# A four-layer convolution sequence: GpSimd's additions wait for the VectorE operation ahead of a port operation, in a new written order

## The chip, the cores and the metric

The kernel runs on one core of a Trainium2 chip. The core has TensorE (matrix products, with a separate path for loading weights), VectorE (elementwise work and scans), ScalarE (activation functions, copies), GpSimd (here: elementwise additions) and SyncE, which issues DMA transfers. The profile calls them PE, PEld, DVE, ACT, POOL and SP. Each engine works through its own queue in order, and waits on semaphores that other engines raise. The metric is the device time of one execution in microseconds (us), as the median of several runs.

## The reference

Four layers work on an input of 4 images of 128 channels x 64 x 64 points, in 32-bit floats:

- Layer 0 is attention over the 4096 points of an image: queries and keys of 16 channels, `softmax(q k)`, values of 128 channels, the result scaled by gamma and added to x.
- Layer 1 is a residual block of two 3 x 3 convolutions (two of the nine taps are masked) with weights and activations quantized to 4 bits.
- Layer 2 is a Mamba block. Two projections to 256 channels, a causal convolution of two taps, `silu`, then a selective scan over the 4096 points with 16 states per channel:

```
h = exp(dt * A) * h + dt * B * x
y = sum over the 16 states of h * C
```

  Then `(y + x D) * silu(z)` is projected back to 128 channels, normalized in groups, put through `silu` and added to the input.
- Layer 3 is attention with 64 channels for queries, keys and values, with an output projection.

## The kernel before

All layers of all four images are in flight together. The work is written as 19 generators ("chains"), such as `energies`, `exponentials`, `products` (attention), `convolutions` (layer 1), `preparation`, `decays`, `scans`, `additions`, `output` (layer 2), `fetches` (DMA). Every step of a chain is one small piece of work on one engine. In which order the steps are issued is written out by hand, as it were: the constant `SCORE` is a string of 9,949 letters, each letter a chain (`n` is `scans`, `o` is `additions`, `i`, `j`, `k` the attention chains). `Order.run` walks through the string and takes the next step of the named chain. The order in which the instructions of one engine are issued follows from this string; the times given to `op(...)` in the code are not used in the kernel (they belong to whatever made the string), and nothing is planned at run time. Attention runs first for images 0 to 2, and in the last stage, layer 3 of image 3, nothing else is left.

Layer 2 is the part that the change touches. It goes in pieces of 512 points (the first two pieces of image 0 have 256). For a piece and two of the 16 states at a time (a "pair"), with both halves of the 256 channels in one tile:

- L1311, on VectorE, multiplies `ud` (dt times x) by the fetched row `b_n` into `hs`, 128 x 2048 elements: the *product*.
- L1285, on ScalarE, makes the decays `exp(dt A)` in PSUM. L1331, on VectorE, is the scan, 128 x 512 elements at a time, two for each state.
- L1348, on VectorE, multiplies `hs` by the fetched row `c_n`: the *readout*. It is issued between the two scans' pairs of the next pair, so that VectorE's pattern is: product, two scans, readout of the pair before, two scans.
- L1359, on GpSimd, adds one state of `hs` to `y`, 128 x 1024 elements: the *addition*, two for each pair. After the 16th state L1363 multiplies `y` by `sz`, the *gating product*.

`hs` has three buffers, so a product waits until the additions of the pair three before are done. `y` has two.

Operations of VectorE marked `port=True` are called *port operations* here: the products and readouts, and in layers 1 and 2 also L938, L950, L977, L984, L987, L1139, L1142, L1144, L1148 and L1226. Right after issuing one of them the code calls `held`, which remembers it. When GpSimd's next addition or gating product is issued, `behind` makes it wait for the remembered operation, by a semaphore. So a GpSimd operation starts only once the last port operation issued before it is done, and runs beside what VectorE does next, in most cases two scans. The calls, at lines 894 to 902, 1311, 1348, 1359 and 1363:

Of the kernel before, what the change touches and what calls it, by code (L numbers as in the profile page):

```python
# [74 lines left out]
    "finish3": "CDEFGHIJ",  # L75
# [4 lines left out]
ittiiuccbvaauitatiaiswjaijaiiukuiviajkajiitkwtiikjijkikcuuisjbbibjkbbittikjjidkikuujiikjibbxcjik  # L80
xxkxbajijabjikkikjjiidxkjayyyykijyieeesejkibjseeiceeceeeekfjkffkijfikffkjjiifdxfjfffxkjxffffpffk
xiixpesfkjkfeffjenlnmlnnfmniinpekfellhmjfnnknenomjoifjkfinhmnlnnmjeifkdlijenpyneylnommjkkihlneyi
eefsnjojknnnflnlhmmffopnnnnfiinkynfkkjiyomlmhjnfpnoonnojlfiknpnjflfmfnonnsmfhkldffnoffkxxnnnxlol
mfppxxnehkfiinenfffejmnnjofekiehlneofmelnjmnnonnikejieneesjflkmeikohjmlnnijpnnijlnophmmnkfflkons
nnodiynijnnyppjmylflfhmkkinjoonnifjfnolflnnnommhnnkfpffkifnnnlnfmhmjokpgonlnnifngjllnfhmfonnnfmn
nikfjffylfmlhpyfmiiokfkdonnonnnnjofkfpfhfknjisljmijfnnonkkploinmnipjjkklnonomnfiikjjhinolkjdfimj
nxnikfxfxxlpnnkxfppjxmoxkkenehenmlijonijeelnmkniijpeeokenhjlnneeeiiemknojnjlfppfnhmkpiodnjinnjfo
kkflkmnnfkflinnmnijhjponppflfmknoniinjogfjklimjgijhnnlkfnokffmndypnpijffnyyfylkkpnyymynflhiejmff
onennokkffijffieejekhkmieelnijnfeenopkinejlmjkndiikjjnloihpneiknjmpnopnklkojpinmfnjikhklnnfomnne
oijflpiknfjkisjfpmdnxjlnmnnoxhpnoiffxjxkkpiljxmiffjnnogklxxmhiisknnojgffkgpennlfefkjifnemopnnejo  # L90
limhiennkjfnpejklnpmfofdiijelnfmkknfnhjoninifjflgnjmnkkijikkjplmpohnifinnonjjkklmnfdijonyffeeffe
ipheenkkjmlnnyykypiiyyojyjffkiijkkknejelopmnnnpmklninhjoiejiipjsdelkjnnompiiknelnhmnffonklnmonnf
fejjkppnfkifpilofmnhnnjjoekflmnzffknnggglpniokotzzzmitudenuxhnelneieeoivmittpfnufuhnmlnpiiwntpit
xxolununxxmfffnflxxmopneheoffffffinnnefeepfelnimtntponeveeesieelomuuniwneefijkhnliifnojjmnijpnln
pkhomiijnneeeejlpkknmnonpkiefelmeeopjnnhfkinijjlmknnkidijmkonlnnfkffsijohljimpnnfjkijkijnoeplenh
pnffmokipljnnoofnfkiimlgnjggkmnknfpnofdyphlnnyfikmfynyoyyjmylpnnonhfnkijjfpfkflmijnonnijlkijkmnn
ophijpkeiiljfkfnmekjonnfpffldmnpoehnnnijiffekifjfpklkjnmnkiikejofnlmphnonnjkiijkjefkofldxnmnijxx
xpnijhlmnkonkiikexjnxxlmonknsijikjjippnlfkjffmennfphijoinlfnmnoefkjlmnhnpopnnofffokidigfkglfmfgp
jnnjhnmfklepoekeiifnnjnpjkelonkimnnpffielojjmkfnffhinijknlonmkdynjeklneepeiyikyyeoyhnmjpnnpyjkif
ylnfoijmkkjneielnihjnkjmiinjjolnmeeeeonnffkfffkpiednppoijjeflkkhnmienenjifkmelpjnokkiijnknjiiljm  # L100
jnhonnklkdmxnpnoijinopjlnkxxxkfmnksxfxpiixhlnnkjmfjofinejnilnjohmnepenoopkfkiiffjlkmffgnkpngeefd
kglnjiiemonhnnepjmoljnkfnfelfkijnfmfnhokifipnnkjipjlmikjfjfkonnnlmfpnfonhkdlnnfeiijmyjeokknlipim
nkpnnojikjhjeenepoilijkjnmnpffiifkffnyyjkyykiydljhmnynkokijifjkklnesjemijonnpnilnmnpfeoekeenpjol
mkiinneknjljepneomkdnxffnepeiijkofxxmfplnxjnkenffxijiopkxxmlknjineljnijpnfkmifonejilkkgmnonnnooj
fgkfmlngeeippnsdelnjmnnpikfoeijfknifjijjfflekkinmonifkfnjklmnnojpffkfnlpiimnonnfjlkndmynjeeioeek
kjlymiyyispenynppkyjjoiikkfjynfffeefnjkfilnjeemneoenkiiljemnkepndkjomlniijhnnpofnkjkilisoenmnjkk
pneofjilmfipjnjhnlnkzfkfmfonnlfpenitkpthimdnxpuxunzxonffiilnvtitxxxiexolzzuumenwimentfitugnounfi
phgngipfgvttfloiggnmniuuoplwffffijnmonghiigjjlnnpknmfnfkoiifeljenmjnnpflhonekepiimfjopnkejlnknii
pkhjmijnjelnonmeeeinoggponffggeffikkfdggkggggggeejglgnjgnkgeeesmgknggeihijkkjlngpgiinokmejknpjlg
nghkpmdnyoiiejjgenijyilkyyykmnegeeynnyfokfijjijkpnkmlnniiheofknjoffjmlnppfinenoijlmknsjfhfnnkoio  # L110
igfdjkjfpmplngkffkgfniglfmhnieefnnjonjiikelekpmoenjnknjlmhoinnpnjifkklfjmopfiidnxnjxnlnmffnjkkox
hfpknpxxxpolmfixnjnijlenphkeomnknijnifjpffkffmiljknknofnpieojeidljhmnnnijeekkkoliijkjmknnnfiflij
jpmhkkeoknnpnildnjmnyioejepnelosypynkiiykyhjmyynkjinijlfkfmjfkffnnpoeeminphoilnkejnffmklnnfjoini
ejlghnjngmnkefoedipnepeoifgslmkfojekknnnpffmeiholjennienkjjemlnfipiojnffkkpnplfhomnjnknieffflkjd
iixnmnonpkjxlxxxnojkxmnxihijjlkefnkkmenonffiifjeeppfjfehknilmknpnionejjijkdlnoijmipnnokkijlifneh
mnnkjjkoeilmeiknkfppnnfjleejsonmnifhniokjjplnfkfmdyinepnijfopljkfyfmkyyhyiinlnfmjnpoyyjneeokgnkk
fgflmgnofhnnfnilimnnjkefpejieiojlmfknnnffhokpnjlmideppiojfkkfjifnnnlnmhjniojlnfmkkiijjkninliksfp
onohmpknnnjjlmokdpnnxfffffnpeikxxxkjijleijmnknhelijoffnexmninkjkijkopnmloijnkhnpnlopkxndmiinxene
jjlnkkiimhnjjkkponepiiflkjknomnenpfjmhfslnnfoknppiijjflkfmfdnynonifljhggmnonnooijikjelyyngyeymne
pikyfyfphlkffnomfnnnelnipofffjmpnjfffehkklnnmenioepneeijlkjnmnoeisijnflkjkidnomhpnneiejjolkfkknm  # L120
nffffkiijefejempepniiplokkhnejnnjezekeflpomknzznnlniimnhvonwliopdxnviminnfwlnfxfimznfhvopenlnfmo
infwxpfifenvhxospmlnnnoofxwlgmingjijpnxxliijgnnmnjhkkkkifofppnikjlkffnmofkipjlfkfnnnhfmnonkfijif
kplnjmokifnnjjkdloidimhjpjennnmelfnkkponkkkknopifjmlhijnfeeijpennfijfflkkkfeokijmnnkkiiddpnjkplj
mehkoiiennnjklpeekknjskmioniCljnhnjiiomnjnfflmnnCkkkokkpjkldpijenifmodhnfnnppjijklomknniienfplkk
fkjmknnhonojklnfiiemknpnjkfjlinhoimnnjppjofkkkfilnmddijnjglengkkkhmnfnonpokfkkflmfpnAiinnjejlehe
mnofnnoijffflmnniiffefkppkjCilkkCChfnCpmnonnooeCkkjjCidCdfgjmklfnnkfffkijijfenhlnkkkminopjepnelo
ikjfCksknDmDniipjkkkenjliioddknjkmpnnpkijlijkjnmkflkiionnmnnjjofkknfplmnnofifjieplnfpfmonnnkjifo
kkojflgfinifpgmkgjfflnmDnonDnnDDDiDjBddilnkkomnDkkklpkmpnojjfnnnfffiljmnifnkkiffoEkEppnjlmonnkkj
pkfflndiijEndikEomjkknknilpEmoEjpiEFjnnnkkkolnFijmnfffjDAffkkinjloiEnEpmfjpnEikknkjiidldmFFkojnn
jnkoklphFmnnnkkiFFiBfjlnFjkkmnFppiiojjlnnkkipjmoinffhknflfnomnkfpjfkdlmhnffioinnnojojlgdgiimnffk  # L130
gppkkjngklggknfpfiomhnjkjnnklnffmiiffnojklkjijmnpfpfFinnAfhofnkkloGGmnnnkddjlnphmofninGGjpplnikk
kkomGkGinGjkjlGmGhijijnnnggpokknfkffkiikfkgjiddlfjkmfHoGnnHnkjlnkoihmpjijnHniiHHkkHHBookflnmpnji
jlgHjmpHnnnohgngkkgggggggpggmgiglkkfkoknnifjfpjggnifidggodlmnfgjkkfnjgkhilgmpnfgpngknoHjfkgkknfo
fiflgfmhnjnifglkgnomjkijfffnlppnmknnionjfkkffpihniddIIlpkmjojIInnhimlnniknpfokjkjnmiiklnfIjnkljk
onphmkkijijnolnniomkppAkkjiIiddIjkknnnlnmnjhfoknpffifIflInijjkkkmnkoiinjjfkklzhmopkknkddnzznittl
noJpiuimulJvinhtInpJtinouuzBiimngJfoJpwntlimtunuJnopnJiolvinmftthniflununpffiomfnwfifjlmnffhngpn
ofglkJnmJijnoffnijlkmhippnnojfijnmknlfffnonijplnhnomnkfkpifjinjfklmiJpjijnkknfdionhlnojippmnjkln
mnkijfionnkjlmikjnknoppffhfnfpijmikjlkfkdnyoinnpijkjijlnikyyyykomynyjiihnkjlefmennjlonmhopkijfkn
neeiienelmjkoppkdijjnnlhmnnokennpkffiiljjonkmffnnpkiljmhionnnpjffikjlmgnfkpfkfnflonmohnnngooikgj
dxffijgmlxikixxxpnkjxknjfxnmlnpipofehjfnneiijkfmpljfinnkojfnfkomlnnfiihnkkjojmlpfdnfnneifffiekkp  # L140
jhmejlfonnneppkiikjijlmjoninneljknkkimikjodnyhlemeneepjenyoyinkyykyijynijkklppnmioneejlhinnjokej
fmfenlpinpneimokjfkffinhnlnojmneijfklnopdmjhnnfifkjnooelnfkfmgkiffigfnmglpkfpenhnnjjlioneeminpjj
kfkfnlonnffpijimnjophneekkldfxonmnfijfnikkxxjiolnmhnixxpknojjlxkxnipimjfnkkfekenlffpfejmeinjlnki
dehjoikffjkknmfenpfopiinneeojlkmihpnnjeiknejjmkipeoljinlnmnknijkjndlhyyyyiioekkmnppyjnjynhloynmk
npofenniijoflkjfpnkmnenifijfjmkpoflhnnijnijfloofkmfnnggkfiihfgdlpkfennjmnfejkeonleomneffflknppni
infkojminjhnoplfinkkjkmnnijliopnfmfnhjplnkdxjnmnoneiexxjliejepekfknoxxkimijxxlenkkeehenfpjffiifk
jkponmnijfnlhmenknijdikofnjlkpijimjennopnlenmkkojheeinnpjmiljpknfonnkiijljkfiknomfnhpjfenedfmyii
lnoknejjyfknfyyyiioyylnppmnkfhnjjelnfmnpofekfgkinglmnniohnffjjmlnnkoepigojieejnelmnfhokfkiniffdj
jefppnlfokfmnnnpkijflnieemkjhfnkiiojneekkejfplffmnkkzzzzndpxiiolvimnxxnnohwfnlviifpxxmownvnnoilp
miwhfnnnivwxxlnpmiiojjiilnnkefkpepnokmnnpolnjjmleeneniikomkjkfkjknnnfifmolnnppejnijlofmnnnoikjkk  # L150
# [37 lines left out]
class Order:  # L188
# [32 lines left out]
    def run(self):  # L221
        for voice in SCORE:
# [7 lines left out]
            if item[1] is None:  # L230
                self.chains.pop(voice)
# [27 lines left out]
def conv_seq_kernel(ctx: ExitStack, tc: tile.TileContext, i: dict, out: bass.AP):  # L259
    nc = tc.nc  # L260
# [1637 lines left out]
```

## Time and profile before

| What | Value |
| --- | --- |
| Median of 3 runs | 3256.88 us (3255.39 to 3258.67) |
| The profiled execution's own time | 3258.73 us |
| Its span, first to last instruction | 3256.9 us |
| Mean granted TensorE clock | 0.983 |
| TensorE busy | 3075.6 us, 94% |
| VectorE busy | 2942.3 us, 90% |
| ScalarE busy | 2550.4 us, 78% |
| GpSimd busy | 1298.7 us, 40% |

A row of a group in the profile reads: line, engine, operation, output and input tiles with their shapes, number of instructions, then after the bar the busy time, the mean of one in ns, and after a second bar the time in which the engine was idle before them, and what ended most of that. A row of waits reads: who waited for whom, in total us, how often, the longest. A row of the timeline reads: start, duration, engine, line, operation, and how many instructions were merged into it. The chain of work that ended last follows the work back from the last instruction.

Busy time is the time in which an instruction is open on its engine. An instruction that has been started and then has to wait for something inside the engine still counts as busy.

### The profile page before, as it was taken

How to read it: one execution, taken by the hardware profiler on the slowest of the kernel's cores; microseconds unless marked ns; L12 is line 12 of the kernel's file. 1: busy time of each engine (PE TensorE's matmuls, PEld its weight loads, DVE VectorE, ACT ScalarE, POOL GpSimd, SP SyncE). 2: the span in 40 equal slices, each digit the busy share in tenths (PEclk: the TensorE clock that was granted, in tenths of full speed). 3: DMA queues.
4: the chain of work that ended last, by engine and by line, in shares of the span. 5: the costliest groups of instructions: out<-in, count | busy, mean ns of one | idle time of the engine just before them, and what ended most of it. 6: DMA issues, size and time to landing. Idle time of an engine off the chain costs nothing. (4 is left out here: it accounts for less than half of the span.)

```text
span 3256.9 us, 69082 instructions
## 1 busy us (share of the span) xinstructions
PE 3075.6 (94%) x29404; PEld 2260.7 (69%) x29404; DVE 2942.3 (90%) x2377; ACT 2550.4 (78%) x3734; POOL 1298.7 (40%) x582
## 2 busy tenths in 40 slices
PE   8989989999899999999898999999899999999998
PEld 7878858888688887555556878865566555565665
DVE  3699999999999999999999999999999999993554
ACT  5888878888788887888787888878888888875554
POOL 0244444444344444444444444444444444450000
PEclk9999999999999999999999999999999999999999
DMA  2233333233333334333333222233333333330000
GB/s 71 81 99 106 102 118 104 96 108 105 108 117 103 104 102 131 105 109 117 111 130 127 99 98 93 97 125 109 104 125 114 133 114 113 119 108 11 2 11 22
DMA packets 134878, 321.67 MB, mean 99 GB/s; under 512 B 44384, under 2 KB 55072, under 8 KB 134560
## 3 DMA queue, kind: packets, MB, share of 16 engines
q1 hardware_dynamic: 134272, 316.32, 28.9%
q8 instruction: 232, 3.80, 0.5%
q10 hardware_dynamic: 288, 0.85, 0.1%
q14 instruction: 86, 0.70, 0.1%
HBM read 300.35 MB, written 16.78 MB: 97 GB/s over the span
## 5 line engine op out<-in xcount | busy, mean ns | idle before, releaser
L1359 POOL TENSOR_TENSOR y<-y,hs 128x1024 f32<-128x1024 f32 (+1 forms) x528 | 1220.0, 2311 | 1569.1 <-DVE hs L1311 644.6
L659 ACT ACTIVATE p<-e 128x1024 f32<-128x1024 f32 x1024 | 1016.4, 1019 | 183.5 <-PE e L641 161.7
L1331 DVE TENSOR_TENSOR_SCAN hs<-da,hlast,hs 128x512 f32<-128x512 f32 (+1 forms) x928 | 1124.7, 1249 | 36.6 <-ACT da L1285 15.8
L723 PE MATMUL us<-v,p 128*128 128x129 f32 x8192 | 1012.9, 280 | 23.7 <-ACT us L780 11.2
L723 PEld LDWEIGHTS us<-v,p 128*128 128x128 f32 x8192 | 964.5, 194 | 81.4 <-ACT p L659 16.8
L1285 ACT ACTIVATE da<-dt,late 128x512 f32<-128x512 f32 (+1 forms) x1056 | 705.5, 677 | 303.4 <-DVE hs L1331 292.0
L1311 DVE TENSOR_TENSOR hs<-ud,b_n 128x2048 f32<-128x2048 f32 (+1 forms) x264 | 620.0, 2348 | 6.3 <-POOL y L1359 4.2
L1348 DVE TENSOR_TENSOR hs<-hs,c_n 128x2048 f32<-128x2048 f32 (+1 forms) x264 | 590.8, 2238 | 4.5 <-DMA c_n<-bc_d 2.3
L641 PE MATMUL e<-it,v 64*128 64x256 f32 x4096 | 531.6, 396 | 21.7 <-ACT p L659 21.3
L732 PE MATMUL us<-p,v 128*32 128x256 f32 x8192 | 501.8, 383 | 4.7 <-ACT p L659 4.1
L641 PEld LDWEIGHTS e<-it,v 64*128 64x128 f32 x4096 | 373.1, 188 | 162.4 <-issue 74.8
L732 PEld LDWEIGHTS us<-p,v 128*32 128x32 f32 x8192 | 246.2, 110 | 216.5 <-issue 53.3
L641 PE MATMUL e<-it,j 64*128 64x256 f32 x2048 | 208.8, 313 | 24.5 <-ACT p L659 19.3
L641 PEld LDWEIGHTS e<-it,j 64*128 64x128 f32 x2048 | 142.7, 186 | 88.0 <-ACT p L659 31.6
L751 PE MATMUL us<-p,ones 128*32 128x256 f32 x3072 | 202.6, 381 | 0.0
L681 DVE TENSOR_TENSOR acc<-p,acc 128x1024 f32<-128x1024 f32 x96 | 117.5, 1224 | 39.3 <-ACT p L659 32.5
L751 PEld LDWEIGHTS us<-p,ones 128*32 128x32 f32 x3072 | 96.1, 110 | 72.9 <-issue 13.2
L1331 DVE TENSOR_TENSOR_SCAN hs<-da,hs 128x512 f32<-128x512 f32 (+1 forms) x128 | 133.2, 1074 | 7.0 <-ACT da L1285 4.4
L1028 PEld LDWEIGHTS <-w 128*128 128x128 bf16 x594 | 53.1, 98 | 85.8 <-issue 43.9
L1028 PE MATMUL xh<-x,w 128*128 128x512 fp8e4 (+1 forms) x396 | 94.7, 375 | 14.0 <-ACT xc L1074 6.7
L1363 POOL TENSOR_TENSOR y<-y,sz 128x1024 f32<-128x1024 f32 (+1 forms) x33 | 75.9, 2301 | 71.4 <-DVE hs L1348 54.8
L681 DVE TENSOR_TENSOR acc<-p 128x1024 f32<-128x1024 f32 x16 | 19.6, 1224 | 83.1 <-PE ss L694 44.4
(173 smaller groups left out, 2563.6 us busy)
## 6 DMA issues: line engine op xcount, KB each, us to landing
b_n<-bc_d SPq DMA_DIRECT2D x256, 512.0 KB, 3.7
c_n<-bc_d SPq DMA_DIRECT2D x256, 512.0 KB, 3.7
x_in<-in_x SPq DMA_DIRECT2D x16, 512.0 KB, 6.1
xpad<-in_x SPq DMA_DIRECT2D x32, 256.0 KB, 4.6
x_d<-yo SPq DMA_DIRECT2D x24, 256.0 KB, 2.1
x_in<-x_d SPq DMA_DIRECT2D x12, 512.0 KB, 5.1
o<-x_d SPq DMA_DIRECT2D x24, 256.0 KB, 4.0
out<-o SPq DMA_DIRECT2D x24, 256.0 KB, 4.2
```

The costliest lines, as they stand in the source:

```text
L641: nc.tensor.matmul(e[h][:, k % 2, k // 4, :], lhsT=jts[s][row : row + D3, col : col + P], rhs=its[s][row : row + D3, c * CB : (c + 1) * CB ...
L659: nc.scalar.activation(p, es[t][h], AF.Exp)
L681: nc.vector.tensor_add(accs[k], ps[t, h], other)
L723: nc.tensor.matmul(us[:, r, 0:VP], lhsT=ps[t, h][:, k % 2, k // 4, r * P : (r + 1) * P], rhs=vts[s][:, 8 * q + k, :], start=q == 0 and k = ...
L732: nc.tensor.matmul(us[m : m + 32, 0, :], lhsT=vts[s][:, 8 * q + k, m % D3 : m % D3 + 32], rhs=ps[t, h][:, k % 2, k // 4, :], start=q == 0 ...
L751: nc.tensor.matmul(us[32 * m : 32 * m + 32, 1, :], lhsT=ones[:, 0:32], rhs=term, start=False, stop=q == NQ - 1 and k >= len(terms) - 4,)
L1028: nc.tensor.matmul(g, lhsT=w3[:, k // len(rhs), lhs[k % len(rhs)] : lhs[k % len(rhs)] + P], rhs=x[:, rhs[k % len(rhs)]], start=(k == 0), s ...
L1285: nc.scalar.activation(da, live["in", g][0][:, h, :], AF.Exp, scale=amat[:, h, n : n + 1])
L1311: held(nc.vector.tensor_mul(hs, live["in", g][1].unsqueeze(1).to_broadcast([P, 2, 2, T]), bcs.pop(("b", k)).unsqueeze(2).to_broadcast([P, ...
L1331: nc.vector.tensor_tensor_scan(hs[:, m % 2, h, :], das.pop((m, h)), hs[:, m % 2, h, :], hlast[:, n, h : h + 1] if index[g] else 0.0, ALU.mult,
L1348: nc.vector.tensor_mul(hs, hs, bcs.pop(("c", k))[:, a:b].unsqueeze(2).to_broadcast([P, b - a, 2, T]))
L1359: behind(nc.gpsimd.tensor_tensor(y, y, hs[:, m % 2], ALU.add))
```

## The change

Two things are changed. First, `held` now remembers two operations: the port operation, and the VectorE instruction issued just ahead of it. A new sign `~` in the string sets `order.early` for the next step; a GpSimd operation issued under that sign waits for the instruction ahead of the port operation in place of the port operation itself. Second, the string is a new one, of 10,350 characters, 401 of them `~`; the other 9,949 name the same steps of the same chains as often as before, but for the voices of one chain (`finish3` now shares its steps among five letters in place of eight), and in another order.

```diff
-    "finish3": "CDEFGHIJ",
+    "finish3": "CDEFG",
...
-ittiiuccbvaauitatiaiswjaijaiiukuiviajkajiitkwtiikjijkikcuuisjbbibjkbbittikjjidkikuujiikjibbxcjik
...
+iCqjiCqqjqiCjijikEkkCjkqqjAiidkrkjkjkidiqCCqqCjjqCiikjqkjkkqqrGCddDDDDDDDDCBDD
...
         self.locks = {True: None, "h": None}
+        self.early = False
...
         for voice in SCORE:
+            if voice == "~":
+                self.early = True
+                continue
             item = self.chains[voice]
...
             if item[1] is None:
                 self.chains.pop(voice)
+            self.early = False
...
     def held(inst):
-        holders[:] = [inst]
+        ahead = next(
+            k
+            for k in reversed(nc.cur_bb.bb.instructions)
+            if k is not inst.ins and k.engine == inst.ins.engine
+        )
+        holders[:] = [ahead, inst.ins]
 
     def behind(inst):
-        for holder in holders:
+        for holder in holders[:1] if order.early else holders[1:]:
             tc.add_manual_dep(
-                inst.ins if hasattr(inst, "ins") else inst,
-                (holder.ins if hasattr(holder, "ins") else holder).name,
+                inst.ins,
+                holder.name,
```

An addition still waits for the readout whose result it adds, so the early wait can only be used when another port operation has been issued after that readout. In the new order 113 additions that stood right behind their own readout have become 72; the others stand one or more port operations later. Of the 401 early operations, 175 are held ahead of a product, 108 ahead of a readout, 118 ahead of the other port operations. The lines of the kernel after the change are higher by 9 to 14 (L1311 is L1325, L1331 is L1345, L1348 is L1362, L1359 is L1373).

## The prediction

> **What bounds the kernel now.** I read the page's busy shares first, then the three stages, then the costliest groups and VectorE's list of waits, and last single stretches in order of time.
>
> ```profile
> PE 3075.6 (94%) x29404; PEld 2260.7 (69%) x29404; DVE 2942.3 (90%) x2377; ACT 2550.4 (78%) x3734; POOL 1298.7 (40%) x582
> ...
> 0.00:112.00 112.00, 102.35 (x815) 87.05 (x816) 43.61 (x119) 70.98 (x97) 2.83 (x19) 1.00 0.23 69
> 112.00:2940.00 2828.00, 2668.77 (x24959) 1973.68 (x24957) 2744.41 (x2099) 2312.74 (x3413) 1295.50 (x564) 0.98 0.33 110
> 2940.00:3257.00 317.00, 304.52 (x3633) 200.02 (x3633) 154.28 (x160) 166.67 (x225) 0.36 (x1) 0.98 0.03 11
> ```
>
> The lower rows are stretches: length, then busy time of TensorE, its weight loads, VectorE, ScalarE, GpSimd. From the first scans (112 us) to GpSimd's last product (2940 us) VectorE is busy for 2744 of 2828 us, 97%, TensorE for 94%. After 2940 us only TensorE is near full. So VectorE sets the pace of the middle, with TensorE close behind; GpSimd is idle half of it.
>
> ```profile
> L1359 POOL TENSOR_TENSOR y<-y,hs 128x1024 f32<-128x1024 f32 (+1 forms) x528 | 1220.0, 2311 | 1569.1 <-DVE hs L1311 644.6
> ...
> ACT da L1285 <- DVE hs L1331: 292.0, 357, 2.9
> ...
> DVE hs L1331 <- ACT da L1285: 20.3, 29, 1.7
> ...
> DVE hs L1311 <- POOL y L1359: 4.2, 24, 0.3
> ```
>
> ScalarE's decays wait 292 us for VectorE's scans, the reverse is 20 us: VectorE leads. What of VectorE's busy time is a hidden wait shows only in time order:
>
> ```profile
> 2515.52 2.26 DVE L1348 TENSOR_TENSOR hs<-hs,c_n 128x2048 f32<-128x2048 f32 x1
> 2517.70 2.45 DVE L1331 TENSOR_TENSOR_SCAN hs<-da,hlast,hs 128x512 f32<-128x512 f32 x2
> 2517.93 2.36 POOL L1359 TENSOR_TENSOR y<-y,hs 128x1024 f32<-128x1024 f32 x1 [2.38 <-DVE hs L1348]
> 2520.07 2.37 DVE L1311 TENSOR_TENSOR hs<-ud,b_n 128x2048 f32<-128x2048 f32 x1
> ```
>
> The readout ends at 2517.78. The addition that waited for it starts 0.15 later and ends at 2520.29, 2.51 after the readout. The two scans beside it end at 2520.15. The next product, recorded from 2520.07, ends 2.29 after the scans, where the first one here ended 2.18 after the scans ahead of it: 0.11 us inside its busy row is a wait for the addition. In every such case it ends 2.15 us after the addition. Summed over all rows of port operations with an addition still running under them, VectorE loses 65.9 us so: 210 waits of up to 0.35 us make 31.4, 27 larger ones 34.5. The larger ones are nearly all a second addition on the same port operation (38 such).
>
> **The change, part by part.** No instruction is added to VectorE (2,379 in both orders), GpSimd has the same 561 additions and products and SP the same DMAs; only semaphore targets and places differ. In the built order 401 of the 561 wait for the operation ahead, 160 still for the port operation (or for nothing of VectorE's).
>
> *What an early wait is worth.* Twice before already, an addition came just after a port operation had begun:
>
> ```profile
> 2573.11 2.27 DVE L1348 TENSOR_TENSOR hs<-hs,c_n 128x2048 f32<-128x2048 f32 x1
> 2573.16 4.44 POOL L1359 TENSOR_TENSOR y<-y,hs 128x1024 f32<-128x1024 f32 x1
> 2577.67 2.36 POOL L1359 TENSOR_TENSOR y<-y,hs 128x1024 f32<-128x1024 f32 x1
> 2578.05 4.13 DVE L1311 TENSOR_TENSOR hs<-ud,b_n 128x2048 f32<-128x2048 f32 x1
> ```
>
> The readout ended at 2575.38, unharmed at its usual 2.27; the addition ended at 2577.60, 2.22 after it. (The other: an addition at 2888.54 took 4.47, the product under it ended at 2890.79, again 2.22.) So an early addition ends 2.22 after its port operation where a late one ends 2.51 after: 0.29 us gained. The next product needs the port two scans later, 2 x 1.17 (median from end to end) + 0.03 = 2.38 after a readout. Late costs 0.13, early nothing, with 0.16 to spare. After a product L1311 the first scan ends 0.21 later than usual (it reads what L1311 wrote), so there even a late addition (2.51) fits before 2.59.
>
> Here the skill speaks against the change: the Trainium skill, "SBUF — State Buffer", section "A bandwidth-pool intuition that's wrong", has GpSimd's blocked work proceed only at "DVE-end + ~115 ns". With 115 ns and then a whole addition of 2.36, it would end at 2.48, 0.03 better than late. The rows say 2.22; I take the rows, and keep the rule as a rival.
>
> *The sum.* I go through both orders, give each port operation its additions and the VectorE work up to the next port operation, with these durations. Before: 208 single additions with small waits 23.7 us, 3 larger 3.3, 28 doubles 37.2: 64.1 us, against 65.9 in the rows, so the account holds. After: 39 late singles 4.3, 6 early ones with a short cover 2.8, 25 of 38 doubles 26.0: 33.1. Saved: 31.0 us of VectorE's time, 19.8 from singles, 11.2 from doubles. By the 115 ns it would be 56.0 left, 8.1 saved.
>
> *The buffer waits.* 24 times L1311 waits 0.16 to 0.28 us for the addition that frees its hs buffer (4.2 us). Before, 52 of the L1311 need an addition held by the very last port operation, all late; after it is 68, of which 13 late. An early one ends at 2.22, L1311 is due at 2.30: hidden if its semaphore takes under 0.08. I take 3 us saved; if not hidden, 55 x 0.1 = 5 lost. Behind a waiting addition stand only further additions and the gating product, and for those wait hs (three buffers) and the output matmul, which has two y buffers.
>
> *What of it reaches the end.* In the part of the chain that the page shows (it begins at 2244 us, so 696 us up to 2940) VectorE has 12% of the span, 391 us, GpSimd 1%, 33: 61%. VectorE's busy share would say 97%. I take three quarters: 34 x 0.75 = 25.5 us. TensorE, at 2669 of then 2803 us, still fits.
>
> *New: an addition that goes first.* By the 2.15 and the unhindered 2.18, a port operation needs its port 0.03 after the operation ahead. An early addition starts 0.08 or 0.14 after it and, being 2.22 long with the port and 2.36 without a wait, reads from 0.14 later still: 0.22 at the soonest. A port operation delayed by more than 0.22 loses, and waits to 2.51. Before, after 112 us, seven of some 750 were late by something other than an addition (0.40 to 2.30, mean 1.03: two of L1139 for ScalarE's logarithm, five readouts for c_n or L1295). 0.9% of 401 is 3.6; I take 5, at 2.51 - 1.03 = 1.5 each, three quarters of it: 6 us back. Bounds: none, and the 30 of a failed plan below.
>
> *The rest of the order.* Up to the first scan both orders have the same work on TensorE to four matmuls. Behind GpSimd's last product the new one has 7 energies (1.93 us per 16), 16 products L732 (3.59 per 64) and 8 sums fewer: 2 us less of the TensorE-bound tail, which the middle hides under VectorE. Table loads rise from 149 to 151, 2 x 1.28 on ScalarE, 82% busy in the middle: hidden, else 3.
>
> Sum: -25.5 - 2 + 6 = -21.5. The profiled execution took 3258.73 with a span of 3256.9; the runs' median is 3256.88, so the span stands for it: **3235 us**, -0.7%.
>
> **Rivals.**
> - *Slower: GpSimd goes first.* A port operation whose semaphore comes over 0.22 us late is shut out up to 2.5 us. It decides at the early waits ahead of readouts (108, most of which wait for L1295 or a fetch) and of L938, L950, L977 (50, by the lines of before). For: those waits exist, and everything on ScalarE comes closer when VectorE is faster. Against: 0.9% in the trace, and L1139, late three times in the whole span, holds no early addition. 27.5 us of gain are used up at 24 losses (1.5 x 0.75 each), 6% of 401; at 10% it is 3257 - 27.5 + 45 = 3274.
> - *No change: the handover is slow.* By the 115 ns: 8.1 x 0.75 + 2 - 6 = 2 us, 3255. Against it are two rows only.
> - *TensorE becomes the bound.* 94% busy and ScalarE's exponentials wait 162 us for energies. With a third let through: 34 x 0.3 + 2 - 2 = 10 us, 3247.
> - *More than the account.* All 34 pass, and the new order takes some 8 of VectorE's 84 idle us as well: 3213.
>
> **How the numbers follow.** Forecast (3222 to 3249) 0.54, more than it 0.12, TensorE 0.09, slow handover 0.09, slower 0.16. Under 0.2% (6.5 us) a measurement can't tell a difference. Faster: 0.54 + 0.12 + 0.09 less 0.01 at its edge = 0.74; same 0.10; slower 0.16. The range leaves a tenth below and the worse half of the slow case above: 3216 to 3263.
>
> **What would show it.** VectorE's L1311 mean down from 2348 to about 2260 ns, L1348 hardly (2238); GpSimd's addition longer, near 4.4 us, since it now waits inside its row; GpSimd's ends 2.22 after the port operations'; VectorE's last readout, now at 2930 us, near 2910. Wrong would be: L1311 or L1348 rows of 4.3 us in numbers over 40; additions that end 2.4 and more after; ScalarE's waits for energies up by what VectorE saved.

## The result and the profile after

The median is 3221.2 us (3214.83 to 3221.84) against 3256.14 us for the kernel before: a ratio of 0.9887, with a 95% interval of 0.987 to 0.9904. That is 35 us, or 1.1%, where 21.5 us were forecast: inside the range, and just under the 3222 us at which the likeliest band of the forecast began. The profiled execution took 3221.84 us with a span of 3220.0 us. The granted clock was a little higher than before (0.986 to 0.990 in the four runs), but the gain isn't the clock's: two runs of the kernel before at 0.987 took 3258.50 and 3258.75 us.

From the page before and the page after: shares, the groups of GpSimd's additions and of VectorE's products (L1325, before L1311) and readouts (L1362, before L1348), each row with its mean in ns behind the busy time. The first two rows are of before.

```profile
L1311 DVE TENSOR_TENSOR hs<-ud,b_n 128x2048 f32<-128x2048 f32 (+1 forms) x264 | 620.0, 2348 | 6.3 <-POOL y L1359 4.2
L1348 DVE TENSOR_TENSOR hs<-hs,c_n 128x2048 f32<-128x2048 f32 (+1 forms) x264 | 590.8, 2238 | 4.5 <-DMA c_n<-bc_d 2.3
...
PE 3048.4 (95%) x29404; PEld 2250.9 (70%) x29404; DVE 2909.4 (90%) x2377; ACT 2550.0 (79%) x3736; POOL 1866.8 (58%) x582
...
L1373 POOL TENSOR_TENSOR y<-y,hs 128x1024 f32<-128x1024 f32 (+1 forms) x528 | 1743.3, 3302 | 994.9 <-DVE hs L1362 411.7
...
L1325 DVE TENSOR_TENSOR hs<-ud,b_n 128x2048 f32<-128x2048 f32 (+1 forms) x264 | 595.7, 2256 | 3.2 <-POOL y L1373 1.4
L1362 DVE TENSOR_TENSOR hs<-hs,c_n 128x2048 f32<-128x2048 f32 (+1 forms) x264 | 590.5, 2237 | 2.4 <-DMA c_n<-bc_d 1.1
```

VectorE's busy time fell by 33 us, from 2942.3 to 2909.4. The product's mean went from 2348 to 2256 ns and the readout's stayed. GpSimd's busy time rose by 568 us with not one more addition: it now waits inside its rows. Its rising share is no load.

A like stretch of the kernel after in order of time, first VectorE, then GpSimd:

```profile
2500.12 2.27 DVE L1325 TENSOR_TENSOR hs<-ud,b_n 128x2048 f32<-128x2048 f32 x1
2502.49 2.46 DVE L1345 TENSOR_TENSOR_SCAN hs<-da,hlast,hs 128x512 f32<-128x512 f32 x2
2504.86 2.27 DVE L1362 TENSOR_TENSOR hs<-hs,c_n 128x2048 f32<-128x2048 f32 x1
2507.05 2.45 DVE L1345 TENSOR_TENSOR_SCAN hs<-da,hlast,hs 128x512 f32<-128x512 f32 x2
2509.41 2.27 DVE L1325 TENSOR_TENSOR hs<-ud,b_n 128x2048 f32<-128x2048 f32 x1
...
2505.09 4.26 POOL L1373 TENSOR_TENSOR y<-y,hs 128x1024 f32<-128x1024 f32 x1 [0.46 <-DVE hs L1345]
```

The addition is released by the scan, is open from 2505.09, 0.23 after the readout's start, and ends at 2509.35. The readout ended at 2507.13, 2.22 earlier. The product that follows ends 2.18 after the scans: nothing hinders it now. Over the trace, 381 of the full-size early operations end behind their port operation, a median of 2.22 us after its end (2.20 to 2.35). One came first, at 2150 us.

Summed as in the prediction, VectorE's hidden waits for the port are 35.0 us, against 65.9 before: 45 small ones of 6.1 us together (210 and 31.4 before), and 29 larger ones of 28.9 (27 and 34.5 before). Products wait 1.4 us for buffers, 4.2 before. "The port" is used here as a name for what a port operation of VectorE and an addition of GpSimd can't have at the same time: in the rows shown, one of the two stands open until the other ends.

The traces can be cut in three: up to the first scan's start, from there to the end of the last readout, and the rest. Times in us; VectorE's busy and idle time are those of the middle.

| Trace | Up to the first scan | Middle | VectorE busy | VectorE idle | Rest |
| --- | --- | --- | --- | --- | --- |
| before | 104.9 | 2828.1 | 2751.1 | 77.0 | 323.9 |
| new order, all late | 109.1 | 2817.8 | 2745.5 | 72.3 | 326.2 |
| the change | 110.0 | 2785.1 | 2716.8 | 68.3 | 325.0 |
| old order, all early | 108.2 | 2800.6 | 2725.7 | 74.9 | 324.5 |

The middle became 43.0 us shorter and the two ends 6.2 us longer. The second and fourth trace belong to the first two experiments below.

### The profile page after: what moved, and what is told of

It is laid out like the page before. It is cut to its first block, busy times and chain, and to the rows that moved or that the text cites. A ratio compares the mean times of both kernels' runs of the same rounds, so it can differ in the third digit from the quotient of the medians.

```text
span 3220.0 us, 69166 instructions
## 1 busy us (share of the span) xinstructions
PE 3048.4 (95%) x29404; PEld 2250.9 (70%) x29404; DVE 2909.4 (90%) x2377; ACT 2550.0 (79%) x3736; POOL 1866.8 (58%) x582
## 5 line engine op out<-in xcount | busy, mean ns | idle before, releaser
L1373 POOL TENSOR_TENSOR y<-y,hs 128x1024 f32<-128x1024 f32 (+1 forms) x528 | 1743.3, 3302 | 994.9 <-DVE hs L1362 411.7
L1345 DVE TENSOR_TENSOR_SCAN hs<-da,hlast,hs 128x512 f32<-128x512 f32 (+1 forms) x928 | 1124.3, 1249 | 33.4 <-ACT da L1299 11.4
L1325 DVE TENSOR_TENSOR hs<-ud,b_n 128x2048 f32<-128x2048 f32 (+1 forms) x264 | 595.7, 2256 | 3.2 <-POOL y L1373 1.4
L1362 DVE TENSOR_TENSOR hs<-hs,c_n 128x2048 f32<-128x2048 f32 (+1 forms) x264 | 590.5, 2237 | 2.4 <-DMA c_n<-bc_d 1.1
L650 PE MATMUL e<-it,v 64*128 64x256 f32 x4096 | 520.7, 392 | 13.4 <-ACT p L668 13.2
L1345 DVE TENSOR_TENSOR_SCAN hs<-da,hs 128x512 f32<-128x512 f32 (+1 forms) x128 | 133.0, 1074 | 12.2 <-ACT da L1299 9.5
L1377 POOL TENSOR_TENSOR y<-y,sz 128x1024 f32<-128x1024 f32 (+1 forms) x33 | 120.8, 3662 | 37.2 <-DVE hs L1345 13.2
L1132 PE MATMUL dt_ps<-xd,late 128*128 128x256 f32 (+1 forms) x264 | 71.3, 393 | 3.9 <-ACT sp L1144 2.8
```

What stands on the lines that cost most here:

```text
L650: nc.tensor.matmul(e[h][:, k % 2, k // 4, :], lhsT=jts[s][row : row + D3, col : col + P], rhs=its[s][row : row + D3, c * CB : (c + 1) * CB ...
L1325: held(nc.vector.tensor_mul(hs, live["in", g][1].unsqueeze(1).to_broadcast([P, 2, 2, T]), bcs.pop(("b", k)).unsqueeze(2).to_broadcast([P, ...
L1345: nc.vector.tensor_tensor_scan(hs[:, m % 2, h, :], das.pop((m, h)), hs[:, m % 2, h, :], hlast[:, n, h : h + 1] if index[g] else 0.0, ALU.mult,
L1362: nc.vector.tensor_mul(hs, hs, bcs.pop(("c", k))[:, a:b].unsqueeze(2).to_broadcast([P, b - a, 2, T]))
L1373: behind(nc.gpsimd.tensor_tensor(y, y, hs[:, m % 2], ALU.add))
L1377: behind(nc.gpsimd.tensor_tensor(y, y, live.pop(("sz", g)), ALU.mult))
```

## The experiments

Each ratio is to runs of the kernel before on the same chip. The experiments ran on several chips, so two of them are better compared by ratios or by the spans of their traces than by medians. "Port waits" is the sum just described, "buffer waits" what products wait for additions by their semaphore; both are from each run's trace.

| Kernel | Median us | Ratio to before (95%) | Span | Port waits | Buffer waits |
| --- | --- | --- | --- | --- | --- |
| before | 3256.1 to 3260.0 | | 3256.9 | 65.9 | 4.2 |
| new order, all late | 3255.9 | 0.9991 (0.9981 to 1.0) | 3253.2 | 65.2 | 6.0 |
| old order, all early | 3235.3 | 0.9921 (0.9904 to 0.9938) | 3233.3 | 38.5 | none |
| new order, 200 early | 3233.1 | 0.9919 (0.9902 to 0.9935) | 3231.5 | 46.0 | 3.7 |
| the change (401 early) | 3221.2 | 0.9887 (0.987 to 0.9904) | 3220.0 | 35.0 | 1.4 |
| the change again | 3222.5 | 0.9896 (0.988 to 0.9913) | 3217.5 | 33.1 | 1.4 |
| new order, all early | 3217.5 | 0.9874 (0.9857 to 0.989) | 3213.5 | 31.1 | none |
| new order, all early, again | 3217.1 | 0.9872 (0.9856 to 0.9889) | 3216.3 | 31.2 | none |
| 19 released too early | 3241.5 | 0.9951 (0.9935 to 0.9968) | 3238.7 | 53.7 | 1.4 |
| additions spread out | 3270.6 | 1.0035 (1.0022 to 1.0047) | 3279.2 | 20.8 | 34.0 |
| new order, tiny additions | 3192.6 | 0.9803 (0.9786 to 0.9819) | 3189.9 | none | none |
| old order, tiny additions | 3195.7 | 0.9811 (0.9794 to 0.9827) | 3193.2 | none | none |

**The new order without the early wait.** Every sign is taken out of the new string.

```diff
-SCORE = new order, 401 "~"
+SCORE = new order, no "~"
```

> The new order, every GpSimd operation waiting for the port operation itself, as before. Theory: the account gives 62.1 us of waits against 64.1 before, and the order may hold some 4 us more, so 3250 (3245 to 3258). Rival, that the gain is in the new order: 3220 to 3235.

It took 3255.93 us, 2.9 under before, with an interval that just reaches no change. So the order alone gives at most some 6 us, and the early wait, on top of it, the rest: 33.2 us by the spans of the two traces, 34 by the ratios. From the page of this run, the product and its share of waiting:

```profile
L1321 DVE TENSOR_TENSOR hs<-ud,b_n 128x2048 f32<-128x2048 f32 (+1 forms) x264 | 608.0, 2303 | 9.2 <-POOL y L1369 6.0
```

The product's mean is between that of before and after, but port and buffer waits together are 71.2 us where before had 70.1: this order had moved loss from products to readouts (2253 ns there) and to the buffers. What it gained in the middle, 10.3 us, it lost in part at the two ends, 6.5. The signs then took 30.2 us of port waits and 4.6 of buffer waits, 34.8 in all. VectorE's own busy time fell by 28.7, which makes 33.3 with the buffer waits, and the span fell by 33.2.

**The early wait without the new order.** The code is that of the change, the string that of before with the sign ahead of every `o`.

```diff
-SCORE = new order, 401 "~"
+SCORE = order of before, "~" ahead of each of the 561 "o"
```

> The order of before, with the early wait for every GpSimd operation (448 take effect; 113 still wait for their own readout). Theory, that VectorE's wait for the port is what the time follows: by the account with 2.22 and 2.51 us the waits fall from 64.1 to 43.4 us, so 3256 - 21 - 2 (buffer waits) = 3233 (3228 to 3242), and GpSimd's early operations end 2.22 us after their port operations. Rival, that an early wait needs a written order that makes it safe: with 20 or more port operations beaten to the port at 1.5 us, 3250 or more. Rival, that the gain is in the new order: 3252 to 3258.

It took 3235.27 us, as the theory had it. An order made for late waits takes the early wait well: in the whole trace one early addition was at its port first (L977 by the lines of before, 2.10 us long at 487 us). The gain is 23.6 us over the kernel before on the same chip, 11 us less than that of the change. In the old order 113 operations still wait for their own readout (72 in the new one), so some 10 us of small waits stay. And of the 31.6 us of waits that went, the span shows only 23.6. Most of the difference lies where no port wait is: the first scan starts 3.3 us later than in the trace of before, at a granted clock of 0.97 in the first 112 us where that trace had 1.00. The middle became 27.5 us shorter.

**Half of the signs.**

```diff
-SCORE = new order, 401 "~"
+SCORE = new order, every other "~" taken out
```

> The change with every other early sign taken out, 200 of 401 early. The account gives 45.0 us of waits against 33.1 with all and 62.1 with none. Theory, that the time follows the waits one to one: 3222 + 12 to 14 = 3235 (3230 to 3240). If three quarters of them pass: 3231. Rival, that the early waits work only as a set (one late addition upsets those behind it): 3245 or more.

At 3233.14 us it lies between 3231 and 3235, and can't tell three quarters from one to one: from this run to the change, port and buffer waits differ by 13.3 us, the spans by 11.5. That the early waits work only as a set is out.

**Every GpSimd operation early.** The new order with the sign ahead of every `o`; 489 take effect.

```diff
-SCORE = new order, 401 "~"
+SCORE = new order, "~" ahead of each of the 561 "o"
```

> The new order, every GpSimd operation with the early wait (489 take effect, 88 more than in the change). Theory: the account gives 30.9 us against 33.1, so 3219 (3214 to 3225), with at most a few port operations beaten. Rival, that the choice of the 401 is what kept it safe: one in ten of the 88 or more beaten at 1.5 us, 3230 or more.

3217.45 us, and no full-size addition was first at the port operation that it is held by. So the 88 further ones cost nothing here. The change and this kernel were run once more:

> The change itself once more, beside the next one on the same chip: 3221 (3215 to 3224).

> The new order with every GpSimd operation early, once more, with more rounds, to place it beside the change: by the account of VectorE's waits (31.1 against 35.0 us in the traces) 4 us under the change, 3217 (3213 to 3221). Rival: the choice of 401 makes no difference, 3219 to 3223.

3222.48 and 3217.11 us, though on two chips and not on one. The traces have 2 to 4 us less of port waits, and it came out lower both times, but the intervals of the ratios overlap: a gain of up to some 5 us over the change is likely and not proven.

**Every twentieth released too early.** In the change, every 20th early operation waits for the instruction two ahead of the port operation. `held` keeps three instructions:

```diff
-        holders[:] = [ahead, inst.ins]
+        holders[:] = [ahead[-2], ahead[-1], inst.ins]
...
-        for holder in holders[:1] if order.early else holders[1:]:
+        which = 2
+        if order.early:
+            order.count_early = getattr(order, "count_early", 0) + 1
+            which = 0 if order.count_early % 20 == 0 else 1
+        for holder in holders[which : which + 1]:
```

> The change, but every 20th early operation (19 take effect) waits for the VectorE instruction two ahead of the port operation, so that GpSimd is at the port first there. Theory: such a port operation waits until the addition is done. With a scan ahead that is 2.51 - 1.17 - 0.03 = 1.3 us (8 of them), with a shorter operation ahead 1.9 (3), behind another port operation 2.2 (8): 33.7 us in all, which pass whole: 3221 + 34 = 3255 (3247 to 3262). If three quarters pass: 3246. Rival, that VectorE isn't shut out by an addition that is there first, or the loss is taken up by other idle time: 3221 to 3230.

3241.52 us, 20 over the change: short of the 34, because only 11 of the 19 took the port. One that did and two that didn't, each with VectorE's rows around it; L1329 and L1366 are this kernel's product and readout, L1005 is another port operation:

```profile
503.21 2.46 DVE L1349 TENSOR_TENSOR_SCAN hs<-da,hlast,hs 128x512 f32<-128x512 f32 x2
505.40 2.36 POOL L1377 TENSOR_TENSOR y<-y,hs 128x1024 f32<-128x1024 f32 x1
505.58 4.32 DVE L1366 TENSOR_TENSOR hs<-hs,c_n 128x2048 f32<-128x2048 f32 x1
...
385.05 1.26 DVE L1349 TENSOR_TENSOR_SCAN hs<-da,hlast,hs 128x512 f32<-128x512 f32 x1
386.18 4.54 POOL L1377 TENSOR_TENSOR y<-y,hs 128x1024 f32<-128x1024 f32 x1
386.22 2.27 DVE L1329 TENSOR_TENSOR hs<-ud,b_n 128x2048 f32<-128x2048 f32 x1
...
2189.46 0.41 DVE L1005 TENSOR_SCALAR x<-q 128x512 fp8e4<-128x512 f32 x1
2189.69 4.62 POOL L1377 TENSOR_TENSOR y<-y,hs 128x1024 f32<-128x1024 f32 x1 [0.29 <-DVE hs L1349]
2189.78 2.29 DVE L1329 TENSOR_TENSOR hs<-ud,b_n 128x2048 f32<-128x2048 f32 x1
```

The first addition starts 0.18 us ahead of the readout and has the port: the readout takes 4.32 and ends 2.14 after the addition. The second starts 0.04 ahead of the product and yet waits, 4.54 in all; the product keeps its 2.27. The third starts 0.09 ahead of the product, but L1005 is still open then, until 2189.87, and the addition stays behind both.

So two cases have to be told apart. With no port operation open when the addition started, six that started 0.17 us or more ahead took the port, and two at 0.04 and 0.05 (386.18 and 2858.05) did not. With one open, it depends on the next one. Four times the next port operation's row began 0.03 to 0.09 us after the end of the open one, and the addition went in between. Four times it began before that end: the addition stayed behind both in three of them (1834.26, 2083.95, 2189.69) and went in between in the fourth (243.78). Why that one differs, these runs don't show.

The 11 that took the port raised port waits from 35.0 to 53.7, by 18.7 us, VectorE's busy time by 18.9 and the span by 18.7. The expectation was wrong in the number of losses.

**One addition for each port operation.** Of the 35 us left, 28.9 are larger waits, and of those 22.4 (21 of 29) stand where two additions are held by one port operation. Here the second is moved behind the next port operation that two scans follow, where nothing needs it sooner; since most of those carry an addition already, 308 places move, mostly by one.

```diff
-SCORE = new order, 401 "~"
+SCORE = new order, "~" ahead of each "o", second "o" of a port operation
+        moved to the next one that two scans follow
```

> The new order, every GpSimd operation early, and second operations on the same port operation moved behind a later one that two scans follow, where nothing needs them before (308 places move, mostly by one). Theory: the account gives 20.8 us against 33.1, so 3209 (3203 to 3217). Rival, that TensorE or the three hs buffers take over as the bound: 3219 or more, with product waits for additions up from 1.4 us to over 10.

It took 3270.6 us, slower than before (the profiled run, at 3281, was the slowest of the six). The port waits fell to 20.8 us just as the account said. What the account doesn't count is the price. VectorE's list of waits of this run, in us, times and longest, and two of the products in order of time:

```profile
DVE hs L1347 <- ACT da L1301: 42.9, 35, 4.0
...
DVE hs L1327 <- POOL y L1375: 34.0, 16, 2.4
...
781.31 2.29 DVE L1327 TENSOR_TENSOR hs<-ud,b_n 128x2048 f32<-128x2048 f32 x1 [2.25 <-POOL y L1375]
1415.08 2.29 DVE L1327 TENSOR_TENSOR hs<-ud,b_n 128x2048 f32<-128x2048 f32 x1 [2.26 <-POOL y L1375]
```

Each addition that is put off holds its hs buffer longer. Products now stand still for up to 2.4 us until a buffer comes free, 34.0 us in all, and the scans wait longer for decays (42.9 us against 19.5 with all early and no move). VectorE's idle time between the first scan and the last readout rose from 67.0 to 141.3 us, and these two waits are 57 of the 74. The doubles can't be spread over three buffers in this way.

**GpSimd out of the way.** GpSimd adds and multiplies one column of each half and leaves out the rest, so the kernel's output is no longer that of the layers. In the new and in the old order:

```diff
-            behind(nc.gpsimd.tensor_tensor(y, y, hs[:, m % 2], ALU.add))
+            behind(nc.gpsimd.tensor_tensor(y[:, :, 0:1], y[:, :, 0:1], hs[:, m % 2, :, 0:1], ALU.add))
...
-                behind(nc.gpsimd.tensor_tensor(y, y, live.pop(("sz", g)), ALU.mult))
+                sz = live.pop(("sz", g))
+                behind(nc.gpsimd.tensor_tensor(y[:, :, 0:1], y[:, :, 0:1], sz[:, :, 0:1], ALU.mult))
```

> The change, with GpSimd's additions and gating products cut to one column of each half (the rest of that work is left out, all waits stay). Theory: the 35.0 us that VectorE still waits for the port and the 1.4 us for buffers go, and all of it passes: 3221 - 36 = 3185 (3178 to 3193). Rival, that TensorE is close under VectorE and takes over: 3200 or more, with ScalarE's waits for energies up. VectorE's products and readouts near 2.20 us each.

> The kernel before, with the same cut of GpSimd's work. Theory: 65.9 us of waits for the port and 4.2 for buffers go, and all passes: 3257 - 70 = 3187 (3178 to 3196), the same as the new order so cut, within the 4 us that the order alone gave. Rival, that the new order is worth more once GpSimd is out of the way: 3195 to 3205. Rival, that TensorE takes over: 3205 or more.

3192.62 and 3195.67 us: the two orders meet within 3 us once the port is free, which is what the order alone had given. Both lie near the upper end of the ranges expected. From the page of the new order so cut, and from its list of waits:

```profile
L1362 DVE TENSOR_TENSOR hs<-hs,c_n 128x2048 f32<-128x2048 f32 (+1 forms) x264 | 582.0, 2205 | 4.2 <-DMA c_n<-bc_d 3.1
...
ACT p L668 <- PE e L650: 157.9, 140, 4.0
```

A readout takes 2205 ns with no addition under it. In the new order 36.4 us of waits went, and the span fell by 30.1; in the old one it was 63.7 for 70.1. In the new order ScalarE waits 158 us for TensorE's energies where it was 138 in the change, and VectorE's idle time in the middle rose from 68.3 to 76.4. That fits TensorE taking a part of the gain from here on, but it isn't shown: ScalarE had waited 162 us in the kernel before.

These two runs also measure what GpSimd costs VectorE without any account. VectorE's busy time fell by 68.5 us in the old order and by 38.8 in the new one, near the 65.9 and 35.0 of the port waits. But the makeup is another. Part of it lies in small operations that the code does not mark as port operations, on one column each, as in the old order with full additions and with tiny ones (shortest, middle and longest duration in ns):

```profile
L1203 DVE TENSOR_TENSOR gd<-gd,mv x4: 159/1186/2219, 883.2 to 2945.4; 128x1 f32<-128x1 f32 x4
...
L1203 DVE TENSOR_TENSOR gd<-gd,mv x4: 159/160/163, 867.2 to 2881.8; 128x1 f32<-128x1 f32 x4
```

An operation of 0.16 us could last 2.2. Such rows held 12.4 us of waiting in the old order and 7.6 in the new, which the port waits leave out. The marked port operations waited less than the sum says, some 54 and 32 us if each is set against the shortest row of its kind.

## Why the prediction was right, and where a size was off

- *VectorE sets the pace of the middle, and loses time inside busy rows to additions.* Shown: with tiny additions both kernels lose 64 and 30 us of span, and VectorE's rows shrink to 2205 to 2211 ns.
- *An early addition ends 2.22 us after its port operation, not 2.51.* Two rows had said so; 381 now do, with the same median. The 115 ns that the prediction kept as a rival stand in the Trainium skill, "SBUF — State Buffer", section "A bandwidth-pool intuition that's wrong (but worth ruling out)", for GpSimd writing DMA descriptors behind a VectorE copy. Carried over to an addition they would have made it 2.48 and left 56 us of port waits. The trace has 35, so that rival is out.
- *The sum of the port waits, 64.1 to 33.1.* The same sum over the rows gives 65.9 to 35.0, a saving of 30.9 for 31.0. In the other orders the account gave 43.4, 62.1, 30.9 and 45.0 where the rows have 38.5, 65.2, 31.1 and 46.0. That it hits so closely is in part luck: the lengths of the marked rows fell by less, about 22 us, and those of the small unmarked operations, which the account had left out, by 5. What VectorE lost to GpSimd fell by 29.7 (68.5 less 38.8). Of the split, small waits gave 25.3 and larger ones 5.6, where 19.8 from single additions and 11.2 from doubles were forecast; the two pairs are not cut in quite the same way, since some doubles make small waits.
- *Buffer waits, 3 us.* 2.8.
- *Three quarters of it reach the end.* This is the term that was mis-sized. Adding the signs to the new order took 33.3 us of VectorE's busy time and buffer waits and 33.2 of the span: all of it. The losing of the port passed whole as well, 18.7 for 18.7. In the old order the middle gave 27.5 for 31.6; from the change to tiny additions it was 30.1 for 36.4. The share of 61% counted only pieces in which VectorE or GpSimd stood in the chain. A likely reason, not tested, is that VectorE's delays are handed on: ScalarE's decays wait for scans, and TensorE's energies for ScalarE.
- *Five port operations beaten, 6 us back.* One was (L964, 2.16 us at 2150 us, 1.8 more than usual), where 1.5 had been forecast for each; the 11 of the experiment cost 1.7 each.
- *The start and the tail.* Equal work up to the first scan had been put at no difference. The scan starts at 110.0 us, 104.9 before. The old order shows both: 104.9 in two traces with a granted clock of 1.00 in the first 112 us, 108.2 in one with 0.97. The change's trace has 0.97 there. So some 3 of those 5 us come with the clock, not with the order. The tail, forecast 2 us shorter, was not: from the last readout's end it is 325.0 us, 323.9 before. The work that had moved out of it was 2 us; where it came back I did not follow.
- *The order alone.* Taken as nothing but that tail; it gave 2.9 us by the medians, with an interval from none to 6. In the traces it is 10.3 us in the middle, 4.7 of them VectorE's idle time, less 6.5 at the two ends.
- *Rivals.* GpSimd first decided nothing; even with every operation early it did not. "More than the account" came nearest, with a chance of 0.12: all the waits passed, and VectorE's idle time in the middle fell by 8.7 us where it had put 8. The total stayed within the range because the ends took 6 us back, which no part of the forecast had in it; that is luck.

## What to carry to other kernels

In this kernel two engines share something that the later one waits for in order, and a wait for the owner's end could be put before the owner's start: the later one then stands ready and ends 0.29 us sooner. Of 401 operations so released, one came first and cost 1.8 us. A busy row can hold a wait. To find how much, set each row against the shortest of its kind, on every operation of the engine and not on the marked ones alone, or take the other engine's work away and see how far the busy time falls. Before moving work away from such a conflict, count the buffers that it holds in the meantime.

## What was unexpected of the hardware

The order of the recorded starts does not quite decide who has the port. With only a scan ahead of it, VectorE's product had the port although an addition had been started 0.04 us sooner (386.18 and 386.22). An addition 0.15 us ahead of a readout took it, in the run with every operation early (2848.90 and 2849.05; the readout took 4.36). The turning point lies between.

Handing the port over was found to cost nothing in either direction: an addition that had waited ended 2.22 us after VectorE's operation, less than the 2.36 it takes on its own, and a product that had waited ended 2.15 us after the addition, less than its own 2.27. And the length of an operation says nothing of how long it may have to wait: one column of 0.16 us stood open for up to 2.2 us.
